# A two-layer graph attention kernel: queries of two tiles by seven quarter-size products, four gather buffers, and s1 carried in the query rows

## Chip, cores and metric

The kernel runs on one core of a Trainium2 chip. The metric is the device time of one execution in microseconds (us), lower is better. The kernel before takes 2733.95 us, the median of three runs (2732.99 to 2736.64).

## What is computed

Thirty-two graphs of 512 nodes with 512 features share one adjacency matrix, in which an entry is 1 with probability 0.0078, about four neighbours a node. Two layers follow each other; each normalises, applies relu, and adds the result of a graph attention to its input. Everything is f32.

```python
h = relu(layernorm(x))
q, k, v = h @ Wq + bq, h @ Wk + bk, h @ Wv + bv          # 8 heads of 64
scores = q.k / sqrt(64) + (1 - adj) * -1e9
x = x + softmax(scores) @ v @ Wo + bo                    # layer 0
h = relu(layernorm(x)); g = h @ W
e = leaky_relu(s1[:, :, None] + s2[:, None, :], 0.2) * adj   # s1 = g @ a1, s2 = g @ a2
x = x + elu(softmax(e) @ g + beta * g)                   # layer 1
```

## The kernel before

**Edges, not matrices.** The kernel doesn't form the 512x512 score matrices. It sorts the nodes once so that each group of 32 has at most 128 edges, and works on edges: a tile is 128 nodes in four groups, so a graph (a "batch" b) has four tiles t. For a tile, keys and values of the neighbours (rows of `tab`, and for b >= 2 the hidden row `hx` of layer 1 of batch b-2 beside them) are gathered by four indirect DMAs into two `kv` buffers (L939), and the queries of the edge's own node from `qtab` by four more into two `qe` buffers (L959). VectorE multiplies and sums per head (L990, L993), ScalarE takes the exponential (L999) and weights the values, 16 small instructions a buffer (L1004), and TensorE adds the edges of a node by products with a one-hot matrix OH (L977, into `px`). This is layer 0 (`layer0`). Layer 1 of batch b-2 (`layer1`) uses the same gathered buffers: `edge_weights` forms z = s1 + s2 per edge (L1109) and from it the matrix `wv`, and L977 sums `hx` rows with it into a `pd` buffer. L977's sums have 32 output columns a group, and four groups share the array.

**Dense products.** TensorE does the rest through six one-bank PSUM buffers `pd` (ring "D") and one double-bank `px`. `turned` transposes 128x128 blocks (L734). `dense` is four matmuls of 128x512 a tile (`product`, L41): hT by Wq for the queries (L787 adds the bias on VectorE), oT by Wo, gT by W. Keys and values of two tiles together come from seven products of half size instead of eight, in `keys_and_values` (L851), in the manner of Strassen and Winograd: VectorE forms the sums S1 to S4 of quarters of the two hT tiles (L840) and the sums of weight quarters once (`right_sums`), and PSUM buffers are reused: ScalarE copies a partial sum (L873, L875) and the next product adds onto the same buffer. L911 and L1071 are column means and sums with 32 output columns.

**s1 in layer 1.** The number s1 of a node is a dot product (L1051). After a batch's layer 0, `self_sums` transposes the batch's s1 (L1080), copies it (L1082), writes it to a DRAM row and reads it back as 128 equal rows (L1088) into a `q` buffer, and picks the entry of each edge by a product with OH and a reduction (L1092, L1093), giving s1e.

**Order.** Every operation is recorded in a list with an engine, a cost in us, a due time (`key`) and the buffers that it reads and writes. `Plan.order` then plays all five engines against each other and emits a fixed order; each engine executes its own list strictly in that order and waits by semaphores. `PACE` scales the listed costs of VectorE (0.9) and ScalarE (0.93) in that play. All rings but the PSUM ones hand out their buffers in the order of due times. GpSimd (POOL) issues all indirect DMAs, rows of x (L759), output rows (L764), and takes the power -1/2 of the normalisation (L746). SP issues the plain DMAs, among them the stores of k, v and q (L890).

Of the kernel before, what the change touches and what calls it, by code (L numbers as in the profile page):

```python
# [9 lines left out]
F32 = mybir.dt.float32  # L10
# [22 lines left out]
HW_ = 520  # L33
ROW = HO + HW_
LAG = 2
DUMMY = 4
# [27 lines left out]
class Plan:  # L64
# [5 lines left out]

    PACE = {"DVE": 0.9, "ACT": 0.93}

# [145 lines left out]
def kernel(  # L218
# [49 lines left out]
    def ring(n, shape, name):  # L268
# [7 lines left out]
        "gT": ring(1, [P, C, P], "gT"),  # L276
        "q": ring(2, [P, D], "q"),
        "k": ring(2, [P, D], "k"),
        "v": ring(5, [P, H, VW], "v"),
        "kv": ring(5, [P, 2, ROW], "kv"),  # L280
        "qe": ring(2, [P, 2, D], "qe"),
        "w": ring(4, [P, D], "w"),
# [10 lines left out]
        "dn": ring(3, [P, 3, T], "dn"),  # L293
        "s1": ring(2, [P, T], "s1"),
        "cs": ring(LAG + 1, [P, C], "cs"),
# [3 lines left out]
        "th": [dram.tile([N + DUMMY, HW_], F32, name=f"th{i}", tag=f"th{i}") for i in range(LAG)],  # L299
        "qtab": [dram.tile([N + 1, D], F32, name=f"qtab{i}", tag=f"qtab{i}") for i in range(3)],  # L300
        "D": [psum.tile([P, D], F32, name=f"pd{i}", tag=f"pd{i}") for i in range(6)],
# [4 lines left out]

    wt2, wt3, wt4 = (wtile([P, C // 2, D], n) for n in ("wt2", "wt3", "wt4"))
    one32 = wtile([P, G], "one32")
    bq_r, bk_r, c_row = (wtile([P, D], n) for n in ("bq_r", "bk_r", "c_row"))
# [14 lines left out]
        "wq", "wk", "wv", "wo", "w1", "rows", "c_row", "wa", "OH", "nzE", "idx", "qidx", "fin",  # L324
        "rmax", "dmax", "bad", "cap", "flag", "perm", "posi", "t1", "t2", "t3", "t4",
    )}

    def setup():
        nc.gpsimd.iota(OH.bitcast(I32), pattern=[[1, D]], base=1, channel_multiplier=0)
        nc.gpsimd.iota(idx[:, 0, 0:1], pattern=[[1, 1]], base=0, channel_multiplier=1)  # L330
        make_identity(nc, ident)
        nc.gpsimd.memset(mhalf, -0.5)
        nc.vector.memset(rings["qe"][-1], 0.0)
        nc.vector.memset(one32, 1.0 / G)
        for b in rings["hx"]:
            nc.vector.memset(b[:, D:], 0.0)
        for b in rings["v"]:
            nc.vector.memset(b[:, :, HD:], 0.0)
        for b in [rmax, dmax, fin]:
            nc.vector.memset(b, 0.0)  # L340

    def constants():

        def load(fn, dma=4096, w=()):
            op("SP", 0.1, 20.0, fn, w=w, dma=dma)

        for dst, src in ((bk_r, bk), (bq_r, bq)):
            load(lambda dst=dst, src=src: nc.sync.dma_start(dst, bcast_rows(src, D)), P * D * 4, [C_["rows"]])
        load(lambda: nc.sync.dma_start(beta_b, bcast_rows(beta, 1)))
        zero = rings["qe"][-1].rearrange("p a b -> p (a b)")  # L350
        for tag, n in (("tkv", D), ("qtab", D), ("th", HW_), ("tab", ROW)):
            for tab in rings[tag]:
                for c0, c1 in ((0, D), (HO, ROW)) if tag == "tab" else ((0, n),):
                    m = 1 if tag == "qtab" else DUMMY
                    load(lambda tab=tab, c0=c0, c1=c1, m=m: nc.sync.dma_start(
                        tab[N:, c0:c1], zero[:m, : c1 - c0]))
        for dst, src in ((bq_c, bq), (bk_c, bk)):
            load(lambda dst=dst, src=src: nc.sync.dma_start(
                dst, bass.AP(tensor=src.tensor, offset=src.offset, ap=[[1, P], [P, C]]),
                allow_slow_non_contiguous=True))  # L360
# [287 lines left out]
    B11, B21, B22, T1 = wk[:, :K2, :], wk[:, K2:, :], wv[:, K2:, :], wv[:, :K2, :]  # L648

    TK = 36.0  # L650

    def right_sums():
# [8 lines left out]
        sub("t2", wt2, B22, T1, lambda c: [(C_["t1"], c), (C_["wv"], K2 + c)], none)  # L661
        sub("t4", wt4, B21, wt2, lambda c: [(C_["t2"], c), (C_["wk"], K2 + c)], none)

    def value_row():
# [117 lines left out]
    def queries(b, t, key, hT):  # L782
        s = st[b]
        p, q = buf("D", "pq"), buf("q", f"q{b}_{t}")
        o = op("PE", 3.43, key, lambda: dense(p.ap, hT.ap, wq), r=[hT, C_["wq"]], w=[p])
        plan.reserve(o, q)
        op("DVE", 0.7, key, lambda: nc.vector.tensor_tensor(q.ap, p.ap, bq_r, op=ALU.add), r=[p, C_["rows"]], w=[q])  # L787
        put(b, lambda: s["qtab"].ap, t, lambda: q.ap, key, q, [(s["qtab"], t)])

    def store_k(b, t, k, key):  # L790
# [40 lines left out]
    def keys_and_values(b, t, key, h0, h1):  # L831
# [52 lines left out]
        store_v(b, t + 0, v[0], key + 0.74 * S)  # L884
        return [(v[i], lambda i=i: v[i].ap) for i in range(2)]

# [9 lines left out]
    def stage_a(b):  # L896
# [3 lines left out]
        for t in range(0, T, 2):  # L900
            keys = [base(T * b + u - AHEAD) if b else 2.0 + 0.4 * S * u for u in (t, t + 1)]
            hT = [turned_state(b, u, key, mv) for u, key in zip((t, t + 1), keys)]
            vs += keys_and_values(b, t, keys[1], *hT) if b else plain_keys_and_values(t, keys, hT)
            for u in range(2):
                queries(b, t + u, keys[1] + (0.28, 0.9)[u] * S if b else keys[u] + 0.56 * S, hT[u])
        key = base(T * b + T - AHEAD) + 0.02 if b else keys[1] + S
# [20 lines left out]
    def stage_b(b):  # L927
# [16 lines left out]
        for t in range(T):  # L944
# [11 lines left out]
            if s is not None:  # L956
                qs = [buf("qe", f"qe{b}_{t}_{i}") for i in range(2)]
                for g in range(NG):
                    op("POOL", 1.3, kb - 0.84 * S + 0.1 * g, lambda q=qs[g // 2], g=g, t=t: nc.gpsimd.indirect_dma_start(  # L959
                        q.ap[:, g % 2, :], None, s["qtab"].ap,  # L960
                        bass.IndirectOffsetOnAxis(ap=qidx[:, t, g : g + 1], axis=0),
                        bounds_check=N, oob_is_err=False),
                       r=[s["qtab"], C_["qidx"]], w=[(qs[g // 2], g % 2)], dma=P * D * 4)
            wvb = edge_weights(b - LAG, t, kb, slots, held) if old is not None else None
            pv = layer0(b, t, kb, slots, held, qs, old is not None) if s is not None else None
# [16 lines left out]
    def layer0(b, t, kb, slots, held, qs, weights):  # L982

        s = st[b]
        for i in range(2):
# [3 lines left out]
            def mult(qe=qe, sl=sl):  # L989
                nc.vector.tensor_tensor(qe.ap, qe.ap, sl.ap[:, :, KO : KO + D], op=ALU.mult)  # L990

            def total(qe=qe, sb=sb):
                nc.vector.tensor_reduce(  # L993
                    sb.ap, qe.ap.rearrange("p n (h f) -> p n h f", f=HD), axis=AX.X, op=ALU.add
                )
# [9 lines left out]

            op("DVE", 1.24, key, mult, r=use([sl], [held[i]], "K"), w=[qe])
            op("DVE", 1.2, key, total, r=[qe], w=[sb])
            op("ACT", 0.25, key, expo, r=[sb, (sl, "use")], w=[held[i]["V"]])
# [54 lines left out]
    def self_sums(b, key):  # L1063
# [5 lines left out]
        def col_sums():  # L1069
# [4 lines left out]
        plan.reserve(o, csr)  # L1074
        op("ACT", 0.6, key, lambda: nc.scalar.copy(csr.ap, pc.ap), r=[pc], w=[csr])
        op("PE", 0.45, key + 0.49 * S, lambda: turned(pt.ap, csr.ap), r=[csr], w=[pt])
        op("DVE", 0.69, key + 0.5 * S, lambda: nc.vector.tensor_reduce(
            cs.ap, pt.ap.rearrange("p (c q) -> p c q", c=C), axis=AX.X, op=ALU.add), r=[pt], w=[cs])
        ps, s1t, row = buf("D", "ps1"), buf("wv", f"s1t{b}"), buf("row", f"row{b}")
# [7 lines left out]

        op("SP", 0.1, key, lambda: nc.sync.dma_start(s1b.ap, row.ap.unsqueeze(0).to_broadcast([P, N])),  # L1088
           r=[row], w=[s1b], dma=P * N * 4)

        def pick():
            nc.vector.tensor_tensor(s1b.ap, OH, s1b.ap, op=ALU.mult)  # L1092
            nc.vector.tensor_reduce(  # L1093
                s1e.ap.rearrange("p t g -> p (t g)"), s1b.ap.rearrange("p (s r) -> p s r", r=G), axis=AX.X, op=ALU.add
            )

        op("DVE", 1.4, key + 0.8 * S, pick, r=[C_["OH"]], w=[s1b, s1e])
        op("DVE", 0.2, key + 0.9 * S, lambda: nc.vector.scalar_tensor_tensor(
            fin, s["mv1"].ap[:, :, 0:2], 0.0, fin, op0=ALU.mult, op1=ALU.add), r=[s["mv1"]], w=[C_["fin"]])
        op("DVE", 0.2, key + 0.9 * S, lambda: nc.vector.tensor_tensor(rmax, rmax, s["rd"].ap, op=ALU.max),  # L1100
           r=[s["rd"]], w=[C_["rmax"]])

    def edge_weights(b, t, kb, slots, held):

# [3 lines left out]
        for i in range(2):  # L1108
            op("DVE", 0.2, k1, lambda i=i: nc.vector.tensor_tensor(  # L1109
                z.ap[:, 2 * i : 2 * i + 2], s["s1e"].ap[:, t, 2 * i : 2 * i + 2], slots[i].ap[:, :, HO], op=ALU.add),  # L1110
               r=[s["s1e"], *use([slots[i]], [held[i]], "H")], w=[z])
        op("DVE", 0.2, k1, lambda: nc.vector.scalar_tensor_tensor(
# [98 lines left out]
    stage_a(0)  # L1211
    right_sums()
    value_row()
    dot_rows()
# [215 lines left out]
```

## Time and profile before

The profiled execution took 2762.45 us; its span from the first to the last instruction is 2760.7 us. The other three runs were not profiled.

| | |
|---|---|
| median of three runs | 2733.95 us |
| profiled execution, its span | 2762.45 us, 2760.7 us |
| granted TensorE clock, mean | 0.989 |
| GpSimd busy | 1824.5 us (66%), 1710 instructions |
| query products (L41, wq), 1024 records | 461.1 us |
| gathers: kv from tab (L939), qe (L959) | 480 and 512, 1.07 and 1.09 us to issue each |
| DMA | 796.71 MB, 289 GB/s |

A "record" is one TensorE instruction: an f32 matmul leaves two, a transpose one. A record's duration runs to the modelled end of the pipeline, so that back-to-back records overlap; the distance between two starts is what one costs. PEld is the loading of weights, which runs beside PE. A group in the list of groups gives line, engine, operation, output and inputs, shapes, count, busy time and mean duration, then the idle time of the engine just before it and what ended that. In the list of waits the three numbers are us in total, times, and the longest.

### The profile page before, as it was taken

The numbers are of one execution on the slowest core, as the hardware profiler recorded it, in microseconds if no ns is written. First come the engines' busy times: TensorE is split into PE (matmuls) and PEld (weight loads), VectorE is DVE, ScalarE is ACT, GpSimd is POOL, SyncE is SP. The second block draws the span as 40 slices with busy tenths as digits, with TensorE's granted clock in tenths as the row PEclk, the third lists the DMA queues.
The fourth block names the chain that finished last, engine by engine and source line by source line (L and its number), as shares of the span: only waits on it lengthen the run. The fifth ranks groups of instructions, "written<-read, shape, count | busy, mean of one in ns | idle before, by whom it ended". The sixth has DMA issues, their size and how long they took to land.

```text
span 2760.7 us, 39873 instructions
## 1 busy us (share of the span) xinstructions
PE 2667.6 (97%) x10250; PEld 1211.9 (44%) x10250; DVE 2089.3 (76%) x5138; ACT 1937.3 (70%) x6245; POOL 1824.5 (66%) x1710
## 2 busy tenths in 40 slices
PE   8999999999999999999999999999999999999876
PEld 4344444444444444444444444444444444444332
DVE  8768878777777677777778778777777777777663
ACT  1557777777767676777767777777777777777763
POOL 2766676676666666666766666766666676666663
PEclk9999999999999999999999999999999999999988
DMA  5988998888888888888888888988988888898863
GB/s 178 283 258 321 315 306 298 309 293 305 303 289 286 298 272 292 302 293 299 301 299 298 304 309 286 325 284 301 325 284 304 302 299 299 304 312 291 302 200 115
DMA packets 242019, 796.71 MB, mean 289 GB/s; under 512 B 35267, under 2 KB 35395, under 8 KB 241782
## 3 DMA queue, kind: packets, MB, share of 16 engines
q0 software_dynamic: 156736, 643.93, 69.5%
q1 hardware_dynamic: 85046, 150.15, 14.8%
q8 instruction: 83, 1.36, 0.2%
q14 instruction: 154, 1.26, 0.1%
HBM read 624.70 MB, written 169.26 MB: 288 GB/s over the span
## 4 chain that ended last, share of the span: by engine, by line
PE 81%; DVE 5%; DMA 5%; ACT 4%; issue 3%; POOL 1%; another core or an unknown queue 0%; SPq 0%; POOLq 0%; DVEq 0%; ACTq 0%
PE pd L41 42%; PE pd L851 24%; PE pd L734 6%; PE pd L977 4%; PE px L977 4%; DMA kv<-tab,idx 3%; ACT kv L1004 2%; DMA x<-in_x_dram,perm 1%; PE pd L911 1%; DVE s L993 1%; DVE qe L990 1%; DMA qe<-qtab,qidx 1%; PE pd L1071 1%; POOL kv L939 0%; DVE w L1051 0%
## 5 line engine op out<-in xcount | busy, mean ns | idle before, releaser
L1004 ACT ACTIVATE kv<-kv 128x64 f32<-128x64 f32 x4096 | 1011.5, 337 | 5.6
L959 POOL DMA_INDIRECT qe<-qtab,qidx x512 | 558.6, 1091 | 273.1 <-issue 115.0
L939 POOL DMA_INDIRECT kv<-tab,idx x480 | 514.8, 1073 | 172.7 <-issue 110.6
L41 PE MATMUL pd<-wo,oT 128*128 128x512 f32 x1032 | 474.2, 603 | 4.7 <-ACT oT L1041 3.6
L41 PE MATMUL pd<-w,gT 128*128 128x512 f32 x1024 | 465.8, 598 | 5.3 <-ACT gT L1162 3.1
L41 PE MATMUL pd<-wq,hT 128*128 128x512 f32 x1024 | 461.1, 593 | 0.0
L759 POOL DMA_INDIRECT x<-in_x_dram,perm x252 | 356.9, 1416 | 90.2 <-issue 57.3
L990 DVE TENSOR_TENSOR qe<-qe,kv 128x1024 f32<-128x1024 f32 x256 | 312.8, 1222 | 49.5 <-DMA kv<-tab,idx 22.8
L993 DVE TENSOR_REDUCE s<-qe 128x16 f32<-128x1024 f32 x256 | 310.5, 1213 | 0.7
L41 PEld LDWEIGHTS pd<-wo,oT 128*128 128x128 f32 x1032 | 198.2, 194 | 252.6 <-issue 236.2
L41 PEld LDWEIGHTS pd<-w,gT 128*128 128x128 f32 x1024 | 195.6, 192 | 251.1 <-issue 235.0
L41 PEld LDWEIGHTS pd<-wq,hT 128*128 128x128 f32 x1024 | 193.7, 190 | 243.1 <-issue 239.6
L764 POOL DMA_INDIRECT out_dram<-w,perm x128 | 149.0, 1164 | 196.5 <-DVE w L1177 140.2
L746 POOL TENSOR_TENSOR mv<-mv,mhalf 128x1 f32<-128x1 f32 x256 | 165.7, 655 | 143.3 <-DVE mv L743 108.8
L851 PE MATMUL pd<-wt,S 128*128 128x512 f32 x496 | 240.2, 607 | 10.3 <-ACT v L873 7.6
L851 PE MATMUL pd<-wk,hT 128*128 128x512 f32 x496 | 239.9, 608 | 4.7 <-ACT kv L999 2.4
L851 PE MATMUL pd<-wv,S 128*128 128x512 f32 x496 | 235.2, 597 | 0.0
L734 PE MATMUL pd<-ident,w 128*128 128x128 f32 x1152 | 161.0, 278 | 32.6 <-DVE w L1028 12.2
L1043 DVE TENSOR_TENSOR x<-pd,x 128x512 f32<-128x512 f32 x128 | 88.0, 688 | 133.3 <-PE pd L41 83.0
L1171 ACT ACTIVATE w<-pd,dn 128x512 f32<-128x512 f32 x128 | 86.7, 678 | 137.8 <-PE pd L41 126.3
L1051 DVE CUSTOM_DVE_ANT_0 w<-hx,wa_r 128x512 f32<-128x512 f32 x256 | 175.5, 686 | 9.8 <-ACT hx L753 5.4
L741 DVE BATCH_NORM_STATS2 st<-x 128x6 f32<-128x512 f32 x256 | 176.2, 688 | 7.3 <-DMA x<-in_x_dram,perm 3.7
(201 smaller groups left out, 3556.0 us busy)
## 6 DMA issues: line engine op xcount, KB each, us to landing
qtab<-q SPq DMA_DIRECT2D x124, 256.0 KB
tab<-hx SPq DMA_DIRECT2D x120, 260.0 KB
tab<-v SPq DMA_DIRECT2D x120, 260.0 KB
tab<-k SPq DMA_DIRECT2D x120, 256.0 KB
qe<-qtab,qidx POOLq DMA_INDIRECT x512
q<-row SPq DMA_DIRECT2D x32, 256.0 KB
kv<-tab,idx POOLq DMA_INDIRECT x480
x<-in_x_dram,perm POOLq DMA_INDIRECT x252
```

The lines of the kernel that those rows point to most:

```text
L41: nc.tensor.matmul(out, lhsT, rhs, start=start, stop=stop)
L734: nc.tensor.transpose(p[:, ts(c, P)], src[:, ts(c, P)], ident)
L741: nc.vector.bn_stats(s6.ap, src.ap)
L759: nc.gpsimd.indirect_dma_start(dst, None, rows, bass.IndirectOffsetOnAxis(ap=perm[:, t : t + 1], axis=0), **lim)
L851: nc.tensor.matmul(p.ap, lhs()[:, c, :], rhs[:, c, :], start=first and c == 0, stop=c == K2 - 1, skip_group_check=True)
L939: nc.gpsimd.indirect_dma_start(dst, None, tab.ap, bass.IndirectOffsetOnAxis(ap=idx[:, t, g : g + 1], axis=0), bounds_check=N + DUMMY - 1, ...
L959: op("POOL", 1.3, kb - 0.84 * S + 0.1 * g, lambda q=qs[g // 2], g=g, t=t: nc.gpsimd.indirect_dma_start(q.ap[:, g % 2, :], None, s["qtab"]. ...
L977: nc.tensor.matmul(out(g), lhs(g), slots[g // 2].ap[:, g % 2, c0 : c0 + n], start=True, stop=True)
L990: nc.vector.tensor_tensor(qe.ap, qe.ap, sl.ap[:, :, KO : KO + D], op=ALU.mult)
L993: nc.vector.tensor_reduce(sb.ap, qe.ap.rearrange("p n (h f) -> p n h f", f=HD), axis=AX.X, op=ALU.add)
L1004: nc.scalar.activation(p[:, h, 0:HD], p[:, h, 0:HD], AF.Copy, scale=p[:, h, HD : HD + 1])
L1051: nc.vector.tensor_tensor_reduce(scr.ap, hx.ap[:, 1 : D + 1], row, 1.0, 0.0, op0=ALU.mult, op1=ALU.add, accum_out=dst)
```

## The change

1. For batches 1 to 31 the queries of two tiles come from `queries_of_two`: seven products of quarter size (two chunks of 128x256) instead of two dense products, with the S1 to S4 of `keys_and_values` and three new matrices qt2, qt3, qt4 made once by `right_sums_q`. The bias of the right half comes by a matmul of a constant matrix, `oneP`, with the bias rows; that of the left half by VectorE. Batch 0 keeps the dense products.
2. The ring "kv" has four buffers instead of five, "k" one instead of two, "s1" three instead of two.
3. Rows of q, qtab and qe have 516 elements. For b >= 2, column 512 of the row holds s1 of batch b-2, and `edge_weights` reads it from the gathered `qe` buffer. The way over a DRAM row remains as `spread_s1` for the last two batches.
4. `PACE` is 1.0 for both engines.
5. The sum of columns in `self_sums` scales by 32 while copying, and reduces 16 of 512 elements.

The core of the diff:

```diff
-    PACE = {"DVE": 0.9, "ACT": 0.93}
+    PACE = {"DVE": 1.0, "ACT": 1.0}
...
-        "q": ring(2, [P, D], "q"),
-        "k": ring(2, [P, D], "k"),
+        "q": ring(2, [P, QW], "q"),
+        "k": ring(1, [P, D], "k"),
...
-        "kv": ring(5, [P, 2, ROW], "kv"),
-        "qe": ring(2, [P, 2, D], "qe"),
+        "kv": ring(4, [P, 2, ROW], "kv"),
+        "qe": ring(2, [P, 2, QW], "qe"),
...
+    def right_sums_q():
+        def sub(name, dst, a, b, r, w):
+            op("DVE", 0.7, TQ, lambda: nc.vector.tensor_tensor(dst, a, b, op=ALU.subtract), r=r, w=w)
...
+        sub("q3", qt3, Q22, Q1, lo + hi, [C_["q3"]])
+        sub("q1", Q1, Q1, Q11, [], lo)
+        sub("q2", qt2, Q22, Q1, lo + hi, [C_["q2"]])
+        sub("q4", qt4, Q21, qt2, [C_["q2"], *hi], [C_["q4"]])
...
+    def queries_of_two(b, t, key, h0, h1, sums):
...
+        def half(kk, p, lhs, rhs, r, first=True, take=None, bias=False):
+            def prod():
+                if bias:
+                    nc.tensor.matmul(p.ap[:, 0:DH], oneP, bq_r[:, DH:], start=True, stop=False, skip_group_check=True)
+                for c in range(K2):
+                    nc.tensor.matmul(p.ap[:, 0:DH], lhs()[:, c, :], rhs[:, c, :], start=first and c == 0 and not bias,
+                                     stop=c == K2 - 1, skip_group_check=True)
...
+        def snap(kk, i):
+            op("ACT", 0.38, key + kk * S, lambda: nc.scalar.copy(q[i].ap[:, DH:D], p1.ap[:, 0:DH]), r=[p1], w=[(q[i], DH)])
...
+        half(0.80, p1, A11, Q11, [h0, *lo], take=q[0])
+        add(0.80, 0, 0, part(p1), bias, [p1, C_["rows"]])
+        half(0.82, p2, A12, Q21, [h0, *hi])
+        add(0.82, 0, 0, part(p2), mine(0, 0), [p2])
+        half(0.84, p1, lambda: S2.ap, qt2, [S2, C_["q2"]], False)
+        snap(0.84, 0)
+        half(0.86, p5, lambda: S1.ap, Q1, [S1, *lo, C_["rows"]], bias=True, take=q[1])
+        half(0.88, p1, lambda: S3.ap, qt3, [S3, C_["q3"]], False)
+        snap(0.88, 1)
+        add(0.88, 1, DH, part(p5), mine(1, DH), [p5])
+        half(0.90, p5, lambda: S4.ap, Q22, [S4, *hi], False)
+        add(0.90, 0, DH, part(p5), mine(0, DH), [p5])
+        half(0.92, p1, A22, qt4, [h1, C_["q4"]], False)
+        add(0.92, 1, 0, part(p1), bias, [p1, C_["rows"]])
+        for i in range(2):
+            if b >= LAG:
+                s1 = st[b - LAG]["s1"]
+                op("DVE", 0.1, key + 0.9 * S, lambda i=i, s1=s1: nc.vector.tensor_copy(
+                    q[i].ap[:, D : D + 1], s1.ap[:, t + i : t + i + 1]), r=[(s1, t + i)], w=[(q[i], "s1")])
+            put(b, lambda: s["qtab"].ap, t + i, lambda i=i: q[i].ap, key + 0.9 * S, q[i], [(s["qtab"], t + i)])
...
-            for u in range(2):
-                queries(b, t + u, keys[1] + (0.28, 0.9)[u] * S if b else keys[u] + 0.56 * S, hT[u])
+            if b:
+                v, sums = keys_and_values(b, t, keys[1], *hT)
+                queries_of_two(b, t, keys[1], *hT, sums)
...
-        op("DVE", 0.69, key + 0.5 * S, lambda: nc.vector.tensor_reduce(
-            cs.ap, pt.ap.rearrange("p (c q) -> p c q", c=C), axis=AX.X, op=ALU.add), r=[pt], w=[cs])
+        op("DVE", 0.2, key + 0.5 * S, lambda: nc.vector.tensor_reduce(
+            cs.ap, pt.ap[:, 0 :: G].rearrange("p (c q) -> p c q", c=C), axis=AX.X, op=ALU.add), r=[pt], w=[cs])
+        if b + LAG >= B:
+            spread_s1(b, key)
...
+            def add(i=i):
+                s1 = s["s1e"].ap[:, t, 2 * i : 2 * i + 2] if qs is None else qs[i].ap[:, :, D]
+                nc.vector.tensor_tensor(z.ap[:, 2 * i : 2 * i + 2], s1, slots[i].ap[:, :, HO], op=ALU.add)
```

## The prediction

> **What bounds the kernel now.** I read four views of the profile in this order: the page (engine shares, chain), the busy time in five stretches, the timeline of TensorE, and the waits of TensorE.
>
> ```profile
> span 2760.7 us, 39873 instructions
> PE 2667.6 (97%) x10250; PEld 1211.9 (44%) x10250; DVE 2089.3 (76%) x5138; ACT 1937.3 (70%) x6245; POOL 1824.5 (66%) x1710
> ...
> PE 81%; DVE 5%; DMA 5%; ACT 4%; issue 3%; POOL 1%; another core or an unknown queue 0%; SPq 0%; POOLq 0%; DVEq 0%; ACTq 0%
> ```
>
> TensorE is busy 97% and is 81% of the chain that ended last. No other engine is over 76%.
>
> ```profile
> 300.00:1350.00 1050.00, 1032.58 (x3978) 466.76 (x3980) 805.62 (x1971) 771.36 (x2508) 708.21 (x661) 1.00 0.87 297
> 1350.00:2570.00 1220.00, 1212.82 (x4731) 555.99 (x4724) 950.47 (x2323) 901.26 (x2917) 827.53 (x773) 1.00 0.87 301
> 2577.00:2760.00 183.00, 136.96 (x529) 58.11 (x521) 101.03 (x286) 102.35 (x311) 102.08 (x95) 0.89 0.62 196
> ```
>
> After the length come PE, PEld, DVE, ACT, POOL, clock, DMA share, GB/s. From 300 to 2570 us TensorE idles 17.4 + 7.2 = 24.6 us: there its work is the time. The tail after 2577 us idles 46 us and is bound by latency; the change leaves its work as it is. So I price TensorE's work first, then its waits.
>
> ```profile
> 41.26 3.85 PE L41 MATMUL pd<-kv,kv 128*128 128x18 f32 x32
> 44.95 2.06 PE L41 MATMUL pd<-wk,hT 128*128 128x512 f32 x2
> ...
> 1011.09 3.60 PE L41 MATMUL pd<-w,gT 128*128 128x512 f32 x8
> 1014.52 3.60 PE L41 MATMUL pd<-wq,hT 128*128 128x512 f32 x8
> 1018.05 1.06 PE L977 MATMUL pd<-kv,wv 128*32 128x512 f32 x8
> ...
> 1022.68 1.04 PE L734 MATMUL pd<-ident,w 128*128 128x128 f32 x8
> 1023.55 0.60 PE L734 MATMUL pd<-ident,x 128*128 128x128 f32 x4
> ...
> 1031.90 1.06 PE L977 MATMUL px<-kv,OH 128*32 128x260 f32 x16
> 1032.89 3.70 PE L851 MATMUL pd<-wk,hT 128*128 128x512 f32 x8
> ```
>
> Price by distance between starts, not by duration. A dense product of a tile is four matmuls, eight records: 1014.52 - 1011.09 = 3.43 us, 0.429 a record of 512 columns. Eight transposes take 23.55 - 22.68 = 0.87 us, 0.109 a record of 128 columns. 18-column products with the same 128x128 weights start about 0.112 us apart, so that is the floor a weight load sets. Entering sums on 32 columns costs 18.05 - 14.52 = 3.53 instead of 3.43; start by start in the trace, entering is 0.522 against 0.429 (+0.093) and leaving 0.313 against 0.200 (+0.113): 0.206 us a round trip.
>
> ```profile
> PE pd L851 <- ACT v L873: 7.6, 7, 3.4
> PE pd L851 <- ACT v L875: 4.5, 4, 2.3
> ...
> PE px L977 <- ACT kv L1004: 2.7, 5, 1.3
> ```
>
> The seven-product method is already used for keys and values, so this shows the price of a **join**: a product that adds onto a PSUM buffer must wait until ScalarE has copied the partial sum. Two joins a pair cost 12.1 us over 62 pairs. Waiting for weighted rows costs 2.7 us.
>
> **What the Trainium skill says.** "TensorE: Matmul & The Clock Gate", Back-to-back issue gap, gives N/2.4 + 2.5 ns with a full clock. The trace agrees if each f32 record streams two cycles a column: 2x512/2.4 + 2.5 = 429, 2x128/2.4 + 2.5 = 109. The same page, LDWEIGHTS, gives columns/1.2 = 107 ns, beside 112 here. "VectorE: DVE Perf Modes", the errata section, gives (N+151)/0.96 ns for an f32 add: 424 ns for 256; L840's 256-column sums take 418 to 420, L859's 512-column adds 686. Its ScalarE row from PSUM, (172+N)/1.2, gives 357 ns for 256; its 570 for 512 is 581 here (L779 584). "PSUM — Partial Sum Buffer", The four PSUM rules, allows a synchronised read within an accumulation group; L873 does that here.
>
> **Part 1, seven products.** For batches 1 to 31, 62 pairs. Removed: 16 records x 0.429 = 6.864 us a pair. Added: seven products of two chunks and one bias matmul, 15 matmuls, 30 records of 256 columns. The trace has no 128x256 dense record. Bounds: 0.214 (half of 0.429, no fixed part) and 0.25 (if a load were partly exposed). I take 0.2157, the line between 0.109 and 0.429, since the load floor of 0.112 lies well below. That is 6.471 us, a gain of 0.393 us a pair, **24.4 us**. The bias matmul is 2 of the 30.
>
> **Part 2, order.** I counted runs of 32-column sums in the two built orders. Before there are 154 entries, after 220: sums that stood together (L977's two kinds, L911, L1071) are now split by quarter products. 66 x 0.206 = **13.6 us lost**. The planner's full durations move later what waits for DVE and ACT; that keeps TensorE from being planned ahead of them. The credit is bounded by 0 and the 24.6 us of idle; I take **10 us gained**.
>
> **Part 3, s1 as a column.** It removes 30 transposes L1080 (0.109 each, **3.3 us**), 30 copies L1082, 60 DMAs on SP, of which L1088 waits 29.7 us for its row at the head of that queue, and 30 picks (L1092 + L1093, 0.683 + 0.686) on DVE. The edge sums (L1109) now wait for the q gather too. Queued behind that wait on DVE is the same tile's multiplication, which needs the same gather; SP and POOL are not behind it. The weights wv are needed only by L977 at the tile's end, so I cost the wait at nothing. If that cover were gone, the pd sums of L977 would wait. The new column copy reads s1 of two batches earlier, finished over a tile before.
>
> **Part 4, DVE and ACT.** DVE: 6 x 0.42 - 2 x 0.686 = +1.15 a pair, +71; 120 column copies at 0.156 (L748's size) +19; picks -41; the smaller reduction L1077 about -16; right sums +3: +36 on 2089, 78%. ACT: 124 copies at 0.37 (page and 581/570) +46, L1082 -8: 72%. Both stay under TensorE, so the work is hidden; not so the joins.
>
> **Part 5, new joins.** Each pair has two more: qt4 waits for ScalarE's copy of the partial sum after qt3, and the last Q22 for a VectorE add that itself waits for this copy. In the built order 49 of 62 pairs have only one group of sums (0.86 us) between qt3 and qt4. Cover: 0.86 + 0.206 - 0.164 (the last record ends 0.593 - 0.429 later than its slot) = 0.90 us, against 0.37 + 0.1 for the copy: 0.4 us is left. Lower bound 0; upper bound about 1 us a pair, if readers come as late as L779, L787 do in this trace (mean 0.8 us behind the product). I take the price of the present joins, **12 us**.
>
> **Part 6, four row buffers.** Along the built order, counting TensorE work, a freed buffer's next sum comes 35 to 39 us later, always; before it was 37 to 66. Needed: four gathers issued in 5.2 us (two in 1.3 x 2 now), landing in 7.1 (10 at most, from the packets), two multiply-and-sum steps 4.9, of which half counts ahead of 2 x 16 weightings at 0.24 = 7.7: about 23 to 26. Slack of 10 us, cost zero; without the cover the wait stands at px <- ACT kv. One k buffer: its two uses lie some ten us apart, a store between; nothing. DMA bytes: 30 x 256 KB less, 16 bytes a row more, -6.6 of 797 MB; nothing.
>
> **Sum.** -24.4 - 3.3 + 13.6 + 12 - 10 = **-12.1 us**. The profiled execution took 2762.45 us (span 2760.7 and 1.8 around it), so 2750; the median of the runs is 28.5 us below that execution, giving **2722 us** (-0.44%). Ramp and tail: +-5.
>
> **Rivals.**
> - **Slower: the joins decide.** qt3, copy, add, Q22 is a chain over three engines with 0.4 us to spare at its first link; ACT executes in order, and ahead of that copy stand mostly relus that wait for statistics through POOL. At 0.5 us a pair 31 us are lost and no order credit comes: 2734 - 14 + 31 = **2751** (2740 to 2775). It decides from 14.1/62 = 0.23 us a pair. For it: the waits of L779 and L1171 on ACT. Against: the present joins cost 0.2 us a pair.
> - **No change: row buffers.** If each of some 120 tiles waits 0.1 us for weighted rows, 12 us: **2734**. For it: all buffers are now reissued only when the tile two back is summed. Against: 2.7 us of such waits now, at 37 us.
> - **The smaller matmul doesn't halve.** At 0.25 a record, 62 x 30 x 0.034 = 64 us lost: **2786**. Against: transposes of 0.109 already hide their loads.
>
> **Numbers.** Forecast 0.55 (own range 2706 to 2728), no change 0.17, joins 0.23, matmul 0.05. Below 0.2% (5.5 us) a measurement here can't tell a change. Range 2706 to 2758: it leaves out the matmul rival, the top of the join rival and a better order, about 0.17 together. Faster 0.55, same 0.17, slower 0.28.
>
> **What would show it.** Right: dense 256-column records start 0.216 apart; eight transposes and dense 512 as before; DVE near 78%; two L1080-like transposes left; entries at 0.2 us. Waits of the query products on ACT's copy and DVE's add near 12 us; over 30 us is the join rival. Waits of px on the weightings over 10 us are the buffer rival. I am wrong if steady idle grows by over 20 us, or falls below 10.

## The result and the profile after

The changed kernel takes **2747.15 us** (median of 7 runs, 2746.20 to 2753.31), the kernel before 2733.95 us beside it (7 runs, 2732.26 to 2741.98). The ratio is 1.0048, 95% interval 1.0033 to 1.0064: it is slower by 13 us, where 12 us of gain were forecast. 2747 us lies inside the whole range that was stated (2706 to 2758), but on the other side of the kernel before.

The execution that was profiled before (2762.45 us) was an unusually long one; a second profile of the same kernel (e1 below, 2741.22 us) is used from here on. Its busy time in two stretches of the steady part and in the tail (length, then PE, PEld, DVE, ACT, POOL, clock, DMA share, GB/s):

```profile
300.00:1350.00 1050.00, 1045.85 (x4079) 475.10 (x4078) 824.45 (x2020) 785.22 (x2557) 724.37 (x676) 1.00 0.88 303
1350.00:2570.00 1220.00, 1209.49 (x4724) 552.34 (x4722) 940.36 (x2299) 894.34 (x2896) 821.74 (x767) 1.00 0.87 300
2577.00:2740.00 163.00, 121.43 (x459) 50.92 (x457) 87.20 (x254) 89.32 (x269) 90.97 (x83) 0.88 0.60 190
```

The page of the changed kernel, profiled at 2746.20 us:

```profile
span 2744.2 us, 42100 instructions
...
PE 2655.9 (97%) x11088; PEld 1369.5 (50%) x11088; DVE 2062.1 (75%) x5391; ACT 1963.1 (72%) x6339; POOL 1780.6 (65%) x1710
...
PE 90%; ACT 2%; issue 2%; DMA 2%; DVE 2%; POOL 2%; SPq 0%; POOLq 0%; DVEq 0%; ACTq 0%
```

And its busy time in the same stretches:

```profile
300.00:1350.00 1050.00, 1049.44 (x4454) 545.82 (x4453) 808.78 (x2124) 790.20 (x2553) 704.12 (x674) 1.00 0.86 301
1350.00:2570.00 1220.00, 1213.98 (x5138) 627.07 (x5137) 935.80 (x2443) 916.50 (x2975) 804.07 (x772) 1.00 0.86 299
2577.00:2740.00 163.00, 114.06 (x440) 51.13 (x429) 85.31 (x247) 86.61 (x264) 91.13 (x83) 0.87 0.59 185
```

TensorE is now busy to within 0.6 us of 1050 and 6.0 of 1220, and makes up 90% of the chain that ended last. So no new wait in the steady part makes the kernel slower. TensorE itself must need more time than was reckoned, or the time is lost at the two ends. Both are the case.

**How the time was split.** For this I laid a nominal distance to the next start beside each TensorE record of a trace: 0.429, 0.216 and 0.109 us for dense records of 512, 256 and 128 columns, 0.112 for the small products, and for the 32-column sums 0.107 us at 512 columns and 0.055 at 260 (four of them share the array; the trace shows 0.43 and 0.22 us for four together). On top come 0.31 us for each entry into these sums, a price that is derived next. What a trace takes beyond that is lost time: "ramp" up to 200 us of such work, "tail" from some 185 us before TensorE's last product to the end, "idle" between. Where exactly the borders lie shifts each of the three by 1 to 2 us.

| | span | work with entries | entries in it | ramp | idle | tail |
|---|---|---|---|---|---|---|
| before (e1) | 2739.4 | 2615.0 | 155 = 48.0 us | 27.6 | 27.2 | 69.7 |
| after | 2744.2 | 2608.1 | 220 = 68.2 us | 39.3 | 12.9 | 84.0 |

The first profile of before gives ramp 28.4, idle 45.3, tail 71.9: what made that execution long stands under idle, while ramp and tail repeat within 2.2 us.

**An entry costs 0.31 us.** TensorE's timeline in the changed kernel (start, length, line, output and inputs, count):

```profile
1016.21 1.88 PE L932 MATMUL pd<-wt,S 128*128 128x512 f32 x4
1017.92 1.88 PE L932 MATMUL pd<-wv,S 128*128 128x512 f32 x4
1019.73 1.07 PE L1066 MATMUL pd<-kv,wv 128*32 128x512 f32 x8
1020.62 1.06 PE L1066 MATMUL px<-kv,OH 128*32 128x260 f32 x16
1021.61 1.98 PE L932 MATMUL pd<-wt,S 128*128 128x512 f32 x4
1023.43 1.03 PE L827 MATMUL pd<-wq,hT 128*128 128x256 f32 x4
1024.29 1.04 PE L754 MATMUL pd<-ident,w 128*128 128x128 f32 x8
```

Read the distances between starts. Four dense records in a row: 17.92 - 16.21 = 1.71 us. Four before a sum: 19.73 - 17.92 = 1.81, so entering costs 0.1. The 16 sums of L1066 take 0.99 instead of 0.88, so leaving costs 0.11. Then comes the part that the prediction doesn't have: the four dense records after leaving take 23.43 - 21.61 = 1.82, again 0.1 too long, though nothing follows them but another dense product. Record by record it is the distance from the first dense record after leaving to the second: 533 ns instead of 429 (or 320 instead of 216); from the second on, the distances are the usual ones. From 300 to 2550 us every exit into a dense product shows it once: 69 of 69 in e1 and 135 of 135 after. An exit into 128-column transposes costs 0.056 there instead of 0.104 (37 exits in e1, 55 after), one into the small transpose L1080 nothing (17 in e1). 0.093 + 0.113 + 0.104 = 0.31 us; averaged over the kinds of exit it is 0.01 to 0.03 less.

The last lines also show the price of the smaller product: four records of L827 in 0.86 us, 0.216 each, as was reckoned. "TensorE: Matmul & The Clock Gate" of the Trainium skill, Back-to-back issue gap, gives the same from two passes of 256 columns (2x256/2.4 + 2.5 = 216 ns).

**The joins don't wait.** The waits of TensorE in the changed kernel (in all, times, longest):

```profile
PE pd L754 <- DVE w L1117: 15.4, 10, 5.5
PE pd L1066 <- ACT w L1269: 14.7, 3, 5.9
PE pd L754 <- DVE w L1249: 12.8, 8, 3.0
...
PE pd L827 <- ACT q L848: 4.5, 2, 3.0
PE pd L1066 <- ACT pd L1270: 4.2, 1, 4.2
```

The two new joins of a pair wait 4.5 us for ScalarE's copy, and in another line 0.9 us for VectorE's add, all within the first 300 us. The waits of the sums L1066 that the profile puts down to ScalarE's L1269 and L1270 are new against e1, and all of them lie after 2554 us, in the tail. What the sums really wait for there is shown below.

### The profile page after: what moved, and what is told of

Its sections match the earlier page's. It is cut to its first block, busy times and chain, and to the rows that moved or that the text cites. A ratio compares the mean times of both kernels' runs of the same rounds, so it can differ in the third digit from the quotient of the medians.

```text
span 2744.2 us, 42100 instructions
## 1 busy us (share of the span) xinstructions
PE 2655.9 (97%) x11088; PEld 1369.5 (50%) x11088; DVE 2062.1 (75%) x5391; ACT 1963.1 (72%) x6339; POOL 1780.6 (65%) x1710
## 4 chain that ended last, share of the span: by engine, by line
PE 90%; ACT 2%; issue 2%; DMA 2%; DVE 2%; POOL 2%; SPq 0%; POOLq 0%; DVEq 0%; ACTq 0%
PE pd L42 32%; PE pd L932 26%; PE pd L827 14%; PE pd L754 7%; PE px L1066 4%; PE pd L1066 4%; ACT kv L1093 2%; PE pd L1160 1%; PE pd L997 1%; PE pd L825 1%; POOL qe L1047 1%; DMA qe<-qtab,qidx 1%; POOL kv L1025 0%; DMA kv<-th,idx 0%; DMA kv<-tab,idx 0%
## 5 line engine op out<-in xcount | busy, mean ns | idle before, releaser
L1093 ACT ACTIVATE kv<-kv 128x64 f32<-128x64 f32 x4096 | 1005.0, 339 | 4.1
L1047 POOL DMA_INDIRECT qe<-qtab,qidx x512 | 517.2, 1010 | 219.7 <-issue 92.1
L1025 POOL DMA_INDIRECT kv<-tab,idx x480 | 533.1, 1111 | 181.2 <-issue 102.4
L1079 DVE TENSOR_TENSOR qe<-qe,kv 128x1024 f32<-128x1024 f32 x256 | 306.9, 1217 | 6.7 <-DMA x<-in_x_dram,perm 5.2
L754 PE MATMUL pd<-ident,w 128*128 128x128 f32 x1152 | 160.4, 278 | 29.5 <-DVE w L1117 15.4
L754 PEld LDWEIGHTS pd<-ident,w 128*128 128x128 f32 x1152 | 132.3, 142 | 103.5 <-DVE w L1117 33.1
L1260 ACT ACTIVATE gT<-pd,cs 128x128 f32<-128x128 f32 x512 | 146.1, 373 | 35.9 <-PE pd L754 33.9
L940 DVE TENSOR_TENSOR v<-pd,v 128x512 f32<-128x512 f32 x124 | 85.1, 686 | 104.2 <-PE pd L932 100.3
L1066 PE MATMUL pd<-kv,wv 128*32 128x512 f32 x1024 | 140.2, 615 | 20.9 <-ACT w L1269 14.7
L766 POOL TENSOR_TENSOR mv<-mv,mhalf 128x1 f32<-128x1 f32 x256 | 146.3, 587 | 16.1 <-DVE mv L763 7.0
```

The source lines that it names most:

```text
L754: nc.tensor.transpose(p[:, ts(c, P)], src[:, ts(c, P)], ident)
L1025: nc.gpsimd.indirect_dma_start(dst, None, tab.ap, bass.IndirectOffsetOnAxis(ap=idx[:, t, g : g + 1], axis=0), bounds_check=N + DUMMY - 1, ...
L1066: nc.tensor.matmul(out(g), lhs(g), slots[g // 2].ap[:, g % 2, c0 : c0 + n], start=True, stop=True)
L1079: nc.vector.tensor_tensor(qe.ap[:, :, 0:D], qe.ap[:, :, 0:D], sl.ap[:, :, KO : KO + D], op=ALU.mult)
L1093: nc.scalar.activation(p[:, h, 0:HD], p[:, h, 0:HD], AF.Copy, scale=p[:, h, HD : HD + 1])
```

## The experiments

Each ratio is to the kernel before, measured beside it on the same chip (its medians there: 2736.5 for e1 to e4, 2737.5 for e5 to e8, 2737.8 for e13 to e16, 2734.6 us for e17 to e19). As these medians differ, gains between runs of different groups are compared by their ratios. Every edit makes the planner draw up a new order, so the price of an edit is that of the edit with the order that came with it.

**e1, the kernel before once more, unchanged.**

> The kernel before, unchanged, profiled once more. Its first profiled execution took 2762 us, 28 us over the median of its runs, with idle stretches of TensorE between 760 and 1350 us. Theory A (that profile was an unlucky execution): this profile shows 2730 to 2742 us, and TensorE idle in 300 to 1350 us under 8 us instead of 17. Theory B (profiling slows the kernel before): about 2760 us again.

2741.22 us in one run. Ramp and tail are those of the first profile within 2.2 us, idle is 18 us less.

**e2, four row buffers alone**, in the kernel before.

```diff
-        "kv": ring(5, [P, 2, ROW], "kv"),
+        "kv": ring(4, [P, 2, ROW], "kv"),
```

> The kernel before with one edit: four gather buffers instead of five. Theory 'buffers' (a round of two tiles through four buffers takes about 36 us; TensorE's work hides it in the steady stretch, not in the ramp and the tail): 12 to 25 us slower than before, all of it in the first 265 us and in the last 200, with tiles of the tail about 18 us apart instead of 15. Theory 'order' (the full durations in the planner cost the time): within 4 us of before. Theory 'work' (entries into 32-column sums decide): within 4 us.

2740.03 us, ratio 1.0012 (1.0006 to 1.0018). With the planner's old paces the price is about 3 us: six entries fewer, idle 7 less, ramp 4 and tail 4 more. The 12 to 25 us of the theory of the buffers did not come.

**e3, full durations alone**, in the kernel before.

```diff
-    PACE = {"DVE": 0.9, "ACT": 0.93}
+    PACE = {"DVE": 1.0, "ACT": 1.0}
```

> The kernel before with one edit: the planner uses full durations of VectorE and ScalarE. Theory 'order': 10 to 15 us slower than before. Theory 'buffers': within 5 us of before, either way; steady idle of TensorE falls towards zero.

2723.59 us, ratio **0.9953** (0.9941 to 0.9966): this one line is worth 13 us. Idle falls from 27.2 to 5.6, and the ramp grows by 7.3. Neither theory had foreseen a gain.

**e4, full durations taken out again**: the changed kernel with the old PACE.

> The changed kernel with the planner's old factors 0.9 and 0.93. Theory 'order': 10 to 15 us faster than the changed kernel, so at or below before. Theory 'buffers': the ramp and the tail stay, and steady idle comes back at the joins of the query products: the same as the changed kernel or up to 20 us slower.

2737.36 us, ratio 1.0003 (0.9995 to 1.0011), against 1.0048: the same line makes the changed kernel 12 us *slower*, as the theory of the order had said. Idle behaves as in e3 (29.5 with the old paces, 12.9 with full durations). But the old order has 170 entries, the new one 220, and 50 x 0.31 = 15.5 us pay it back. Ramp and tail together are 8 us longer with the new order, so the spans differ by 6.6; the rest of the 12 lies in which executions were profiled, and in the two chips.

**e5, fewer entries.** The planner adds STAY to the rank of an operation that would change between dense products and 32-column sums.

```diff
-    STAY, WAIT = 1.0, 0.2
+    STAY, WAIT = 3.0, 0.2
```

> The changed kernel with one planner constant: leaving or entering the 32-column sums costs 3 instead of 1 in the choice of the next TensorE operation. The order has 147 entries into such sums instead of 220. Theory 'entries' (a round trip costs 0.31 us, since the second record after leaving takes 0.10 us more as well): 73 x 0.31 = 23 us faster than the changed kernel, about 2724 us. The price of the prediction, 0.206, gives 15 us: 2732. Theory 'buffers alone' (ramp and tail by four buffers and the late weights): within 5 us of the changed kernel.

2724.70 us, ratio 0.9957 (0.9941 to 0.9972). 147 entries instead of 220: 73 x 0.31 = 22.6 us. The medians fell by 22.5, and by the ratios the gain is 24.9 us, with some 6 us of uncertainty. At 0.206 it would have been 15.

**e6, s1 by a DRAM row for all batches**, as before, in the changed kernel.

```diff
-QW = 516
+QW = 512
...
-            wvb = edge_weights(b - LAG, t, kb, slots, held, qs if s is not None else None) if old is not None else None
+            wvb = edge_weights(b - LAG, t, kb, slots, held, None) if old is not None else None
...
-        if b + LAG >= B:
-            spread_s1(b, key)
+        spread_s1(b, key)
```

> The changed kernel with s1 brought over the DRAM row again for all batches and query rows of 512 elements; products, four buffers and full durations stay. 211 entries. Theory 's1 column' (the edge weights wait for the q gather, which delays the sums of layer 1 at the end of each round, where TensorE's work doesn't hide it): ramp and tail 10 to 20 us shorter, 2727 to 2737 us. Theory 'buffers' or 'entries': 0 to 5 us slower than the changed kernel, since 30 transposes and picks return; within 3 us with the 9 entries fewer.

2750.23 us, ratio 1.0047 (1.0034 to 1.006): no change in the whole. In its parts, the tail is 8.8 us shorter (75.2), and ramp (43.5) and idle (21.7) are 13 longer. Ramp and tail together are 4.6 us shorter, where the theory of the column said 10 to 20.

**e7, dense products for the queries again**, all else as changed.

```diff
-                queries_of_two(b, t, keys[1], *hT, sums)
+                for u in range(2):
+                    queries(b, t + u, keys[1] + (0.28, 0.9)[u] * S, hT[u])
```

> The changed kernel with the dense query products; s1 column, four buffers and full durations stay. 142 entries. By TensorE's work alone: 24.4 us come back and 78 x 0.31 = 24.2 us go, so the same time as the changed kernel (2747) if ramp and tail belong to the buffers or to the s1 column. If the quarter products, with their chain of copies and adds, make the ramp and the tail, about 2725 us.

2736.41 us, ratio 0.9999 (0.9991 to 1.0008): the products, meant to save 24 us, cost 13 by the ratios. The order without them has 142 entries, with them 220: 78 x 0.31 = 24.2 us. Their whole gain goes into the entries. The spans differ by another 8 us: with the products idle is 6.6 and the ramp 3.2 longer, the tail 2.0 shorter.

**e8, three of the other edits without products and column**: full durations, four row buffers, one k buffer in the kernel before.

> The kernel before with full durations (2723.6 us so far) and with four gather buffers and one k buffer. 185 entries instead of 151. Theory 'buffers': 34 x 0.31 = 10.5 us of entries and 8 to 12 us in ramp and tail, 2742 to 2746 us. Theory 'entries' alone: about 2734 us. If neither costs: 2724 us.

2745.60 us, ratio 1.0030 (1.002 to 1.004), against 0.9953 in e3: 185 entries instead of 151 (10.5 us), and the tail 77.0 instead of 67.0.

**e13, s1 as a row for the last stage alone**, with the STAY of e5.

```diff
-            wvb = edge_weights(b - LAG, t, kb, slots, held, qs if s is not None else None) if old is not None else None
+            wvb = edge_weights(b - LAG, t, kb, slots, held, qs if b < B - 1 else None) if old is not None else None
...
-        if b + LAG >= B:
+        if b + LAG >= B - 1:
```

> The changed kernel with stay 3 (as in e5), and with s1 brought as a row of 128 for the tiles of the last stage alone (all else keeps the column). 148 entries into 32-column sums, against 147 in e5, so the steady part should be that of e5 (2724.7 us, 0.9957 of the kernel before). Theory that the column of s1 lengthens the tail, because the weights wait for the gathered rows where TensorE no longer covers it: 7 to 9 us less than e5, 2716 to 2718 us, 0.9925 to 0.9935, with the tail at some 74 instead of 82 us. Rival, that the tail's growth is that of the four row buffers alone: no change from e5, 2723 to 2726 us, tail 80 or more.

2723.20 us, ratio 0.9946 (0.9933 to 0.9959), not to be told from e5. The tail is 83.4: the column's reading in the last stage alone isn't what lengthens it. That theory fell.

**e14, five row buffers with the column**: e7 with kv 5.

> The kernel of e7 (dense products for the queries, s1 as a column, full durations, one k buffer) with five buffers for gathered rows instead of four. 141 entries against 142 in e7. Theory that four buffers cost time at the two ends, where a tile waits for the buffer of two tiles before: e7's tail of 86 us falls by 4 to 10 us and the time from 2736.4 to 2727 to 2732 us (0.9965 to 0.9985). Rival, that the buffers cost nothing once s1 comes as a column (both waits run side by side): 2735 to 2737 us (0.9995 to 1.000).

2736.63 us, ratio 0.9999 (0.9991 to 1.0007), as e7. Tail (81.9 after 86.0) and ramp (33.2 after 36.1) are a little shorter, idle 4.3 longer. With the column, the fifth buffer doesn't bring the tail of e3 (67.0) back either.

**e15, a middle dose of entries**: STAY 2, 182 entries.

> The changed kernel with stay 2 instead of 1: 182 entries into 32-column sums, between the 220 of the changed kernel and the 147 of e5. Theory that an entry costs 0.31 us: 38 fewer than the changed kernel, 11.8 us less, 2735 us (0.9995 to 1.001 of the kernel before). With the predicted 0.206 us: 7.8 us less, 2739 us (1.002). If what made e5 faster was another property of its order and not the count: anything from 2724 to 2747 us, off the line between the two.

2740.51 us, ratio 1.0009 (1.0001 to 1.0016). From the ratio 1.0048 that is 10.7 us for 38 entries, 0.28 each. But the intervals of the two ratios leave 6 to 15 us, 0.16 to 0.41 each, so this run doesn't tell 0.206 from 0.31. In us it lies above the 2735 expected; its idle is 3.0 and its ramp 3.9 more than in the changed kernel, while the count took 11.8.

**e16, five row buffers and STAY 3**, with the room taken from other rings (x1 8, w 3, S 2).

> The changed kernel with stay 3 and five buffers for gathered rows; the room is taken from other rings (x1 8 instead of 9, w 3 instead of 4, S 2 instead of 3). 172 entries, 25 more than e5, so 7.8 us more by that count: 2732.5 us. Theory that four buffers cost 4 to 10 us at the two ends: 2722 to 2728 us. Rival, that they cost nothing, or that the other rings now hold the tail: 2732 us or more.

3056.47 us, ratio 1.117 (1.1154 to 1.1187). 326 us of idle stand in the steady part, where TensorE now waits for many different things; which of the three smaller rings is to blame was not separated. It says nothing on the row buffers.

**e17 and e18: one k buffer alone, and four row buffers alone**, each with full durations in the kernel before.

> The kernel before with full durations and one k buffer (five row buffers, dense queries, s1 by row). 151 entries, as in e3. Theory that the single k buffer costs nothing at the two ends: as e3, 2722 to 2726 us (0.995), ramp 35, tail 67. Rival, that it and not the row buffers lengthened e8's tail (77): tail 75 to 77, 2731 us or more.

> The kernel before with full durations and four row buffers (two k buffers, dense queries, s1 by row). 187 entries, 36 more than e3, so 11 us more by count. Theory that the four row buffers alone lengthen the tail: tail 75 to 79 as in e8, time 2743 to 2748 us (1.002 to 1.004). Rival, that it was the k buffer: tail 67 to 69, time 2734 to 2737 us.

e17 takes 2723.67 us, ratio 0.9960 (0.9947 to 0.9972), tail 67.0: one k buffer costs nothing here. e18 takes 2753.01 us, ratio 1.0071 (1.0043 to 1.0098), tail 77.5, 188 entries. That is above the 2748 us expected. So with full durations the four row buffers alone cost 29 us. The spans differ by 27: 37 entries are 11.5, the tail 10.5 and idle 8.6, less 3.5 of ramp.

**e19, the changed kernel once more.**

> The changed kernel once more, nothing edited. If ramp and tail belong to the order of the instructions and not to the execution, they repeat within 3 us: ramp 36 to 42, tail 81 to 87, time 2745 to 2750 us. If they are chance, they fall anywhere between those of the kernel before (28, 70) and these.

2747.75 us, ratio 1.0046 (1.0031 to 1.0061). The tail repeats (83.6); the ramp is 44.1 instead of 39.3, outside what was expected.

**The walk from before to after**, one edit at a time:

| kernel | ratio | entries | ramp | idle | tail | lag |
|---|---|---|---|---|---|---|
| before (e1) | 1 | 155 | 27.6 | 27.2 | 69.7 | 23.1 |
| + full durations (e3) | 0.9953 | 151 | 34.9 | 5.6 | 67.0 | 23.0 |
| + four row buffers (e18) | 1.0071 | 188 | 31.4 | 14.2 | 77.5 | 33.5 |
| + one k buffer (e8) | 1.0030 | 185 | 32.2 | 9.7 | 77.0 | 36.9 |
| + s1 as a column (e7) | 0.9999 | 142 | 36.1 | 6.3 | 86.0 | 41.4 |
| + seven products (after) | 1.0048 | 220 | 39.3 | 12.9 | 84.0 | 37.8 |

("Lag" is explained next; the step to e7 also has the third s1 buffer and the smaller sum of columns.) The steps in time are not prices of the edits: one k buffer takes 11 us off between e18 and e8 (by the ratios), and nothing in e17 against e3. What repeats from order to order is the tail. With full durations, one k buffer and dense queries it is 67.0 us with five row buffers and s1 by row (e17), 77.0 with four buffers (e8), 81.9 with the column (e14) and 86.0 with both (e7). So each of the two lengthens it, the column more, and their effects don't add up.

**What the lag is.** It is the time from the start of TensorE's last product of the last batch's normalised rows to VectorE's first multiplication of that batch's gathered rows. From there to the end the kernels of the table need nearly the same, 155 to 162 us (before 162.2, after 161.0; e2, with the old paces, 149.7 after a lag of 38.7). The lag grows by 14.7 us from before to after, the tail by 14.3. This suggests that the tail's growth is there before the last stage begins, and it fits that e13, editing only that stage, changed nothing. It isn't shown: in e2 the lag is 38.7, and the tail only 4 us longer than before. GpSimd's timeline shows what holds the gathers up. First e17, five buffers and no column (in brackets the idle time before, and what ended it):

```profile
2545.30 1.01 POOL L959 DMA_INDIRECT qe<-qtab,qidx  x1 [0.31 <-issue]
2546.61 1.01 POOL L959 DMA_INDIRECT qe<-qtab,qidx  x1 [0.30 <-DMA tab<-v]
2547.94 1.14 POOL L939 DMA_INDIRECT kv<-tab,idx  x1 [0.32 <-issue]
2549.38 1.00 POOL L939 DMA_INDIRECT kv<-tab,idx  x1 [0.30 <-issue]
...
2555.45 1.05 POOL L959 DMA_INDIRECT qe<-qtab,qidx  x1 [0.76 <-DVE z L1109]
```

Two gathers of queries, two of rows, and so on: the halves of a tile alternate. The last product there was at 2539.0, the first multiplication of the batch came at 2562.0. In the changed kernel (2545.3 and 2583.2):

```profile
2564.39 1.04 POOL L1025 DMA_INDIRECT kv<-tab,idx  x1 [3.48 <-PE px L1066]
...
2567.60 1.01 POOL L1025 DMA_INDIRECT kv<-tab,idx  x1 [0.30 <-issue]
2568.91 1.93 POOL L1025 DMA_INDIRECT kv<-tab,idx  x1 [0.30 <-issue]
2571.15 0.99 POOL L1025 DMA_INDIRECT kv<-tab,idx  x1 [0.30 <-issue]
...
2573.77 1.05 POOL L1047 DMA_INDIRECT qe<-qtab,qidx  x1 [0.31 <-DVE z L1210]
```

The first gather waits until the sums of an earlier tile have freed its buffers, the other three stand behind it, and the queries come only then, all four in a row. And in e14, with five buffers but the column:

```profile
2540.24 0.99 POOL L1023 DMA_INDIRECT kv<-tab,idx  x1 [0.31 <-PE pd L1158]
2545.52 1.00 POOL L1045 DMA_INDIRECT qe<-qtab,qidx  x1 [4.29 <-DVE z L1204]
2546.83 1.00 POOL L1045 DMA_INDIRECT qe<-qtab,qidx  x1 [0.30 <-issue]
```

Here the query gather waits for L1204 (L1206 of the changed kernel), the edge sum z that now reads its column from the `qe` buffer. VectorE's earlier reduction of a `qe` buffer (L1080 at 2540.21) had ended at 2541.42, and the gather still waited until the edge sum at 2545.11: the column keeps the buffer taken for longer. (In e17 the last line names an edge sum too, but that one doesn't read `qe`; there a reduction of `qe` ended at the same time, 2555.16.) Four buffers alone (33.5, 36.9) or the column alone (e14: 36.2) are each enough for a lag of some 35 us; both together give 35 to 41. So undoing the buffers (e14 against e7) brings 4 us of tail back, and undoing the column for all batches (e6 against after: lag 32.1) 8.8, of 19 that both cost. How the gathers bring this about rests on one profile of each kernel; what was not tried is the changed kernel with five buffers and s1 by row. e16 had to take the room for its fifth buffer from other rings.

**What the sums wait for in the tail.** All engines in the changed kernel, shortly before the longest wait of the sums L1066:

```profile
2588.83 0.16 DVE L1210 SCALAR_TENSOR_TENSOR z<-z 128x4 f32<-128x4 f32 x1
...
2590.87 5.82 ACT L1093 ACTIVATE kv<-kv 128x64 f32<-128x64 f32 x24
...
2596.60 0.19 ACT L1212 ACTIVATE z<-z 128x4 f32<-128x4 f32 x1
...
2597.16 0.28 DVE L1219 TENSOR_TENSOR wv<-OH,z 128x128 f32<-128x128 f32 x1
```

The edge sum z was ready at 2588.99, but its exponential (L1212) stands in ScalarE's list behind the weightings of the gathered rows (L1093) and runs at 2596.60. From it VectorE forms the weights wv, which are ready at 2597.44, and the sums start at 2597.55, 0.11 us later. In all five waits of these sums after 2554 us they start 0.06 to 0.11 us after wv has ended, so wv is what they wait for, whichever line the profile names. These waits take 20.7 us in the changed kernel (14.7 + 4.2 + 1.8), 7.5 in e1 and none in e17.

## Why the prediction was wrong

By its own terms, after against e1, in us:

| term | predicted | found |
|---|---|---|
| seven products | -24.4 | -23.8, at 0.216 a record |
| transposes L1080 | -3.3 | -3.3 |
| entries | +13.6 | 65 x 0.31 = +20.2 |
| new joins | +12 | 5.4 of waits, all before 300 us; not a row of its own, as they stand under ramp and idle |
| order | -10 | idle -14.3 |
| ramp | 5 either way | +11.7 |
| tail | 5 either way | +14.3 |

Without the joins these add up to +4.8, the difference of the two spans. The medians differ by 13.2; the execution of e1 lay 3 to 7 us above the medians of its kernel, and that of after 1 us below. As a long execution shows itself in idle, the credit against a median execution is nearer to 6 to 10 us (14.3 less 3 to 7, less 1). What the forecast missed, then, is 26 us of ramp and tail and 6.6 of entries; what it priced and didn't come is the 12 us of joins.

- **Part 1 was right**, though it was the riskiest price: half the columns take half the time. The rival of a matmul that doesn't halve is refuted. (The 0.112 us that it took for the floor of a weight load is none: the transposes in its own lines start 0.109 apart, each with a load of its own.)
- **Part 2 failed in a size: "66 x 0.206".** The round trip was read at its two borders, where the starts next to the sums are. The third part lies one record further in, between the first dense record and the second. The traces show it, and the gain of e5 agrees with the full price. That the entries would rise was right, and so was the count.
- **Part 2's credit left out its price.** Full durations took 17 to 22 us of idle (e4 to after, e1 to e3), of which the rest of the change gave some back. On the changed kernel they also chose 50 entries more (e4), so that they cost time there. Steady idle from 300 to 2570 us fell to 0.6 + 6.0 = 6.6 us, below the 10 that the prediction had named as a sign of being wrong.
- **Part 5 failed, and with it the rival that pointed to the right side.** Its mechanism isn't what happened; that its 2751 us lies near the measured 2747 is luck. After 300 us no query product waits for a join. ScalarE's copy takes 366 ns and VectorE's adds 416 to 420, as reckoned, and the planner knew both and put other products between; idle fell instead of rising. Charging the new joins with the waits of the old ones (L873, L875) was unfounded: those waits came from the shortened durations. They are 8.7 us in e1 and 0.4 us in e3, which differs in the durations alone.
- **"Cost zero" of the four row buffers failed.** The slack of 10 us was counted in TensorE work along the order, which is a cover only where TensorE has that work to do. At the end it has not, and the edge work comes 10 us later (e18 against e3), with a tail that is 10 us longer (e8 against e17, e18 against e3). 37 entries more came with them in the order of full durations (e18), but six fewer with the old paces (e2), so that part belongs to the order that the planner happens to find.
- **"I cost the wait at nothing" of Part 3 failed at the same place.** The column alone lengthens the tail by 15 us (e14 against e17), and by 9 where there are four buffers already (e7 against e8, after against e6). The sign that Part 3 itself had named came: without the cover, the pd sums wait, 20.7 us in the tail against 7.5. The queue behind the wait was examined on VectorE, but not ScalarE's, where the exponential of z stands behind the weightings, nor the buffer that the column keeps: `qe` is now released by the edge sum.
- **"Ramp and tail: +-5" failed**: together +26. This and the entries turn the sign. The tail's share is traced above. The ramp's is not settled: 7.3 of the 11.7 us are there in e3, with full durations alone, but e4, with the old paces, has a ramp of some 35 us too, and it varies by 5 us between two profiles of the same kernel (e19).
- Part 4 counted six VectorE adds a pair, where the kernel has five. VectorE ended at 2062.1 us (75%) instead of near 78%; as TensorE waits for it only 1.1 us from 300 to 2554 us, nothing hangs on this.
- The kernel is slower than the no-change rival by the same 13 us; that rival had the right suspect, the row buffers, but in the steady part, where between 300 and 2554 us no wait of L1066 is found.

The clock adds to the tail of both kernels, and nearly alike: it is 0.88 in the last stretch of e1 and 0.87 in that of the changed kernel. In the changed kernel the sums L1066 at 2597.55 follow 5.87 us of idle:

```profile
2597.55 2.05 PE L1066 MATMUL pd<-kv,wv 128*32 128x512 f32 x8 [5.87 <-ACT w L1269]
2599.23 2.11 PE L1066 MATMUL px<-kv,OH 128*32 128x260 f32 x16
```

They take twice what they take at 1019.73. "TensorE: Matmul & The Clock Gate" of the Trainium skill, Part 1 on the clock gate, says that TensorE falls to half its clock after an idle window of about 3.4 us and needs a busy one to return; the trace agrees with half the speed after 5.87 us. But in e1 the same sums (L977 at 2632.53) take 2.05 us after 2.85 us of idle already, so 3.4 us is no safe bound here.

**Versions that beat both kernels:** full durations alone (e3, 0.9953; e17, with one k buffer, 0.9960) and the changed kernel with STAY 3 (e5, 0.9957; e13, 0.9946). Their intervals overlap. So the products, with all that came along to make room for them, have shown nothing beyond what one line of the planner gives. Not tried was STAY 3 without the products, in the kernel before with full durations or in that of e7, so what the products are worth under it stays open.

## What to carry to other kernels

Price a change of matmul shape over several records on both sides, not at the border alone, and count how often a new, finely divided product lets the planner split what stood together: here 78 more entries ate the whole gain of 24 us. Judge a buffer's slack by the work that covers it, and look at the place where that cover ends, such as the last batch. And when a value is moved into another buffer, ask who releases that buffer now.

## What the runs showed of the hardware

After a stretch of 32-column sums, the second dense f32 record starts 0.104 us late behind the first, whether the first has 512 columns (533 ns from start to start instead of 429) or 256 (320 instead of 216); behind a 128-column transpose it is 0.056 us. This comes on top of 0.093 us for entering and 0.113 for leaving. Its cause isn't shown.
